# Cross-attention and feed-forward block: the attention loop taken in beats of two key blocks, with the subtraction of maxima and the sums of denominators on other engines

## The chip, the cores and the metric

The kernel runs on one NeuronCore of a Trainium2 chip. The metric is the device time of one execution in microseconds (us). In the profile the engines are PE (TensorE: matmuls; PEld is its loading of stationary operands), DVE (VectorE), ACT (ScalarE), POOL (GpSimd) and SP (SyncE). Each engine works through its own queue in program order. DMAs that add to what lies at their destination are issued from POOL's queue here.

## The reference, cut to what matters

All tensors are float32 with one batch. `x` is 2048 x 256, the context 1601 x 256 with a mask over its rows, and there are 4 heads of 64.

```python
latents = _layernorm(x)
xn, ln = layernorm(ctx, ln_x_g, ln_x_b), layernorm(latents, ln_l_g, ln_l_b)
q  = ln @ W_q
kv = concatenate([xn @ W_kv, ln @ W_kv], axis=1)      # 1601 + 2048 keys
qn, kn = rmsnorm(q, q_gamma) * 64 ** -0.5, rmsnorm(k, k_gamma)
sim  = where(full_mask, qn @ kn.T, -finfo.max)        # per head; latents are never masked
attn = softmax(sim)
x = x + (attn @ v) @ W_out + b_out
y = _layernorm(x)                                     # no gains
h = bit_linear(y, w1)                                 # rows to int8 steps, weights to -1, 0, 1
h = silu(depthwise_conv1d(h, conv_w, conv_b))         # 3 taps along the sequence
x = x + bit_linear(h, w2)
```

## The kernel before

A prologue (lines 207 to 409) normalizes context and latents, makes keys `kT` (two heads on the two halves of the partitions), values `v_sb` and queries `qT`, and looks ahead at the scores of the first unit. The middle is the attention loop. The end is the feed-forward part in slots (lines 794 to 963).

**Units and blocks.** A unit is 512 queries (of 2048, index `g`) and a pair of heads (`pr`): 8 units, numbered 0 to 7 here. Keys come in 29 blocks of 128: 13 of context (0 to 12, the last one padded) and 16 of latents (13 to 28). A tile of one unit and one block is 128 keys x 2 heads x 512 queries, [128 x 1024] float32.

**Softmax.** It needs each query's maximum before any exponential. So while unit u runs, `look_ahead` makes the scores of unit u+1 (`sa`, in PSUM) and DVE reduces each tile to maxima over 32 keys at a time (`mxs`). Context blocks are kept: ACT copies them to SBUF with the mask added (`sg`, in a ring of 14). Latent blocks are dropped and made again in unit u+1. At a unit's end `column_maxima`, `transpose_maxima`, `row_maxima` and `spread_shift` join the maxima (`m`, `tpm`, `nm`) and split their negatives in two bfloat16 parts (`hi`, `val`, `rows`). A matmul of `rows` with ones then spreads them over all key partitions (`sh`), and ACT copies that to SBUF (`nb`).

In unit u+1 a kept block gets its shift by `subtract` (`sg + nb`, on DVE). A latent block gets it on PE: `again` puts the bfloat16 matmul of `rows` into PSUM and adds the scores to it (`st`). `exponential` (ACT) makes `pt` in SBUF, in a pool of 5, two steps ahead. `attend` multiplies with the values into `ot`, one PSUM bank that all blocks of a unit add to. Every score matmul uses one half of the array's rows for each head, every product with values one half of its columns; the profile writes these as 64*128 and 128*64.

**PSUM.** Score tiles (`sa`, `st`, `sh`) share three buffers of two banks (`big`). One bank is for `ot`, one (`bank`) for everything small.

**Denominators.** Sums of `pt` over blocks are kept in two tiles. POOL adds context blocks and the last two blocks to `acc`; DMAs issued on POOL's queue add the other latent blocks to `acd` (in the last unit, DVE). `finish_unit` copies `ot` out (ACT) and puts small pieces on a plan by step: `join` the sums (POOL), eight matmuls to columns (`dn`), inverses (DVE), eight diagonal matrices (`dg`, ACT), eight matmuls that spread them again (`rd`), and the division (DVE).

**Order.** All four engines are held in program order (`InOrder`, lines 157 to 170). The loop runs over 8 x 29 steps of one block each. `order` takes a latent block in even steps and a context block in odd ones, then the last three latent blocks. `early` says which block of the next unit is looked ahead to in which step. After a query group's second unit, `finish_block` plans for each of its four blocks of 128 rows: bias (POOL), projection (`po`, PE), residual and statistics (DVE, `mv`), inverse deviation (two steps on POOL), normalization, quantization (DVE), transposes (`tpq`, PE) and a copy to `xq_all` (ACT). These pieces fall into units 2, 4, 6 and, for the last group, into the feed-forward slots. In the last unit `weight_tasks` load and quantize the feed-forward weights.

Of the kernel before, what the change touches and what calls it, by code (L numbers as in the profile page):

```python
# [17 lines left out]
P = 128  # L18
# [8 lines left out]
def kernel(  # L27
# [386 lines left out]
    def at(k, *calls):  # L414

        plan.setdefault(k, []).extend(calls)
# [30 lines left out]
    with att:  # L447
# [13 lines left out]
        def transpose_maxima(m4):  # L461
            tp = bank("tpm", [P, P])
            tensor.transpose(tp, m4.rearrange("p a b -> p (a b)"), ident)
            return tp

        def row_maxima(tp):
# [6 lines left out]
            vector.tensor_copy(hi, nm)  # L473
# [24 lines left out]
        def subtract(u, j):  # L498

            vector.tensor_tensor(staged[u, j], staged[u, j], shifts[u][1], ALU.add)  # L500
# [13 lines left out]
        def attend(u, j, pt, ot, sums, i):  # L514


            g, pr = units[u]
            acc, acd = sums
            if j < NCB or i >= NKB - 2:
                if j == 0:  # L520
                    gpsimd.tensor_copy(acc, pt)
                else:
                    gpsimd.tensor_tensor(acc, acc, pt, ALU.add)
            elif u == len(units) - 1:
                if i == 0:
                    vector.tensor_copy(acd, pt)
                else:
                    vector.tensor_tensor(acd, acd, pt, ALU.add)
            elif i == 0:
                gpsimd.dma_start(acd, pt)  # L530
            else:
                gpsimd.dma_start(acd, pt, accum_op=ALU.add)
            for hh in range(2):
# [3 lines left out]
                    start=(i == 0), stop=(i == NKB - 1),  # L537
                )

        def finish_unit(k, ot, sums, dst):  # L540

            scalar.copy(dst, ot)
# [6 lines left out]
            def denominators():  # L549

                box["dn"] = bank("dn", [P, NSUB, 2])
                for sub in range(NSUB):
                    for hh in range(2):
                        tensor.matmul(
                            box["dn"][:, sub, hh : hh + 1], acc[:, hh, ts(sub, P)], ones[:, 0:1],
                            start=True, stop=True,
                        )

            def inverses():
                box["r"] = sm.tile([P, NSUB, 2], F32, tag="r", name="r", bufs=2)  # L560
                vector.reciprocal(box["r"], box["dn"])

            def diagonals():
                box["dg"] = ptp.tile([P, NSUB, 2, P], F32, tag="pt", name="dg")
                for sub in range(NSUB):
                    for hh in range(2):
                        scalar.activation(
                            box["dg"][:, sub, hh, :], ident, AF.Copy,
                            scale=box["r"][:, sub, hh : hh + 1],
                        )  # L570

            def spread_inverses():
                box["rd"] = bank("rd", [P, NSUB, P])
                for sub in range(NSUB):
                    for hh in range(2):
                        tensor.matmul(
                            box["rd"][halves(hh), sub, :], ones[:, :DH], box["dg"][:, sub, hh, :],
                            start=True, stop=True,
                        )

            def divide():
                vector.tensor_tensor(
                    dst, dst, box["rd"].rearrange("p s q -> p (s q)"), ALU.mult
                )

            for n, call in (
                (1, join), (3, denominators), (4, inverses), (5, diagonals), (6, spread_inverses),
# [149 lines left out]
        for k in range(AHEAD + 1):  # L737
            if kept(k):
                subtract(*steps[k])
# [257 lines left out]
```

## Time and profile before

| what | value |
|---|---|
| median of 3 runs | 1016.02 us (1014.09 to 1018.25) |
| the profiled execution: its own time, its span | 1019.8 us, 1018.0 us |
| mean granted PE clock | 0.899 |
| busy PE, DVE, ACT, POOL | 859.8, 819.0, 523.0, 537.6 us |
| DMA queue of POOL (software_dynamic) | 51.39 MB, 25.8% of 16 engines' span |

A group's line has the engine, the operation, what it writes and reads with shapes, the count, busy time and mean, and the idle time just before with what ended it. Nearly all lines of the attention loop and the end carry L165, the helper that holds the order, so groups are told apart by their tiles. In a timeline the first two columns are start and length in us; a matmul's length includes its way through the array, so the time that one takes from the next is the difference of their starts. One float32 matmul shows as two records: `x4` is one tile for both heads.

### The profile page before, as it was taken

What the parts mean: (1) busy time and instruction counts of PE and PEld (TensorE: products, weight loads), DVE (VectorE), ACT (ScalarE), POOL (GpSimd) and SP (SyncE); (2) the same over time, 40 slices, a digit from 0 to 9 for tenths busy, and PEclk for the clock granted to TensorE, in tenths of its full rate; (3) what the DMA queues carried; (4) which work ended last, traced back from release to release, by engine and by line L of the source; (5) the groups of instructions that cost most, each with busy time, mean ns of one, the idle gap of its engine ahead of it and who ended that gap; (6) DMA issues with size and microseconds to landing.
All of it is one profiled execution on the core that took longest, in us unless ns stands there. A gap on an engine that the chain in (4) does not pass through costs nothing.

```text
span 1018.0 us, 10253 instructions
## 1 busy us (share of the span) xinstructions
PE 859.8 (84%) x3672; PEld 323.7 (32%) x3672; DVE 819.0 (80%) x946; ACT 523.0 (51%) x706; POOL 537.6 (53%) x415
## 2 busy tenths in 40 slices
PE   4788978998998999899899999989998877555543
PEld 3334532222322333232233323223332323333321
DVE  4566447996898689779868998977898995799996
ACT  2456444554654644455454566556554435755560
POOL 2432343556555556646655675646566546545431
PEclk9999998999999999899989999999998897556565
DMA  5010002453444344245534335544344000000000
GB/s 133 21 33 10 1 0 58 87 104 80 86 91 97 83 83 82 62 84 99 109 75 79 75 83 104 96 92 98 69 84 102 22 0 21 1 11 11 21 10 32
DMA packets 29775, 63.28 MB, mean 62 GB/s; under 512 B 7259, under 2 KB 16668, under 8 KB 29724
## 3 DMA queue, kind: packets, MB, share of 16 engines
q0 software_dynamic: 14112, 51.39, 25.8%
q1 hardware_dynamic: 12030, 10.44, 3.3%
q10 hardware_dynamic: 3582, 0.79, 0.4%
q8 instruction: 29, 0.48, 0.2%
q14 instruction: 22, 0.18, 0.1%
HBM read 9.13 MB, written 2.10 MB: 11 GB/s over the span
## 4 chain that ended last, share of the span: by engine, by line
PE 53%; DVE 36%; ACT 5%; issue 2%; POOL 2%; DMA 2%; ACTq 0%; POOLq 0%; DVEq 0%
PE sa L165 15%; PE ot L165 15%; PE st L165 10%; DVE mxs L165 6%; DVE sg L165 5%; PE kv L353 5%; DVE t L165 4%; DVE m L165 3%; PE sa L179 3%; DVE acd L165 2%; DVE y L165 2%; DVE h L165 2%; DVE hi L165 1%; DVE rows L165 1%; DVE hq L165 1%
## 5 line engine op out<-in xcount | busy, mean ns | idle before, releaser
L165 POOL TENSOR_TENSOR acc<-acc,pt 128x1024 f32<-128x1024 f32 x112 | 283.2, 2529 | 36.0 <-ACT pt L165 35.5
L165 PE MATMUL ot<-pt,v_sb 128*64 128x512 f32 x928 | 254.2, 633 | 2.0 <-ACT pt L165 1.9
L165 DVE TENSOR_TENSOR sg<-sg,nb 128x1024 f32<-128x1024 f32 x104 | 218.2, 2104 | 14.1 <-ACT nb L165 14.1
L165 PE MATMUL sa<-q_un,kT 64*128 64x512 f32 x812 | 223.9, 640 | 3.0 <-DVE mxs L165 3.0
L165 POOL DMA_DIRECT2D acd<-pt x98 | 84.0, 857 | 214.6 <-ACT pt L165 156.9
L165 ACT ACTIVATE sg<-sa,maskc 128x1024 f32<-128x1024 f32 x91 | 101.2, 1112 | 177.1 <-PE sa L165 176.9
L165 ACT ACTIVATE pt<-st 128x1024 f32<-128x1024 f32 x128 | 130.9, 1023 | 77.4 <-PE st L165 77.3
L165 DVE TRANSPOSE_TENSOR_REDUCE mxs<-sa 128x32 f32<-128x1024 f32 x112 | 137.2, 1231 | 34.4 <-PE sa L165 33.6
L165 DVE TRANSPOSE_TENSOR_REDUCE mxs<-sg 128x32 f32<-128x1024 f32 x91 | 112.7, 1238 | 40.8 <-ACT sg L165 40.8
L165 PE MATMUL st<-q_un,kT 64*128 64x512 f32 x512 | 141.8, 633 | 0.0
L165 ACT ACTIVATE pt<-sg 128x1024 f32<-128x1024 f32 x104 | 109.3, 1051 | 41.9 <-DVE sg L165 41.9
L165 PEld LDWEIGHTS sa<-q_un,kT 64*128 64x128 f32 x812 | 64.0, 186 | 138.7 <-issue 88.3
L165 PEld LDWEIGHTS ot<-pt,v_sb 128*64 128x64 f32 x928 | 48.8, 139 | 183.8 <-issue 174.1
L165 POOL TENSOR_TENSOR side<-side,t 128x512 f32<-128x512 f32 x32 | 40.6, 1270 | 48.8 <-DVE t L165 47.8
L165 PEld LDWEIGHTS st<-q_un,kT 64*128 64x128 f32 x512 | 53.4, 202 | 34.9 <-issue 31.1
L165 ACT ACTIVATE t<-h,cb_sb,cw_sb 128x256 f32<-128x256 f32 x64 | 37.9, 591 | 38.6 <-DVE h L165 38.6
L353 PE MATMUL kv<-wkv_sb,feat 128*128 128x512 f32 (+1 forms) x116 | 55.5, 620 | 0.0
L165 PE MATMUL st<-rows,ones 64*128 64x512 bf16 x256 | 52.4, 403 | 1.5 <-DVE mxs L165 1.5
L329 DVE TENSOR_TENSOR nn<-raw,ss 128x512 f32<-128x512 f32 (+1 forms) x23 | 15.7, 681 | 47.0 <-POOL ss L101 47.0
L165 PE MATMUL py<-w2T,hq 128*128 128x256 bf16 x128 | 30.2, 417 | 26.4 <-DVE hq L165 26.4
L101 POOL TENSOR_TENSOR ss<-ss,neg_half 128x8 f32<-128x8 f32 (+1 forms) x23 | 37.7, 1638 | 1.9
L97 POOL TENSOR_SCALAR ss<-ss 128x8 f32<-128x8 f32 (+1 forms) x23 | 5.8, 253 | 60.2 <-DVE ss L320 60.1
(130 smaller groups left out, 1001.1 us busy)
## 6 DMA issues: line engine op xcount, KB each, us to landing
acd<-pt POOLq DMA_DIRECT2D x98, 512.0 KB, 4.5
tok<-in_x_dram SPq DMA_DIRECT2D x4, 512.0 KB, 3.5
q_un<-in_x_dram SPq DMA_DIRECT2D x4, 512.0 KB, 3.6
w_sb<-in_L_ffn_w_dram SPq DMA_DIRECT2D x4, 512.0 KB, 3.2
out_dram<-res SPq DMA_DIRECT2D x16, 128.0 KB, 1.8
tok<-in_ctx_dram SPq DMA_DIRECT2D x3, 512.0 KB, 4.1
wkv_sb<-in_L_xattn_W_kv_dram ACTq DMA_DIRECT2D x1, 512.0 KB, 9.0
wo_sb<-in_L_xattn_W_out_dram SPq DMA_DIRECT2D x1, 256.0 KB, 8.8
```

The costliest lines, as they stand in the source:

```text
L97: gpsimd.tensor_scalar(x, x, floor, None, op)
L101: gpsimd.tensor_tensor(x, x, e, ALU.pow)
L165: return tc.keep_in_program_order(getattr(self.engine, name)(*args, **kwargs))
L179: tensor.matmul(st[:, hh, :], kT[halves(hh), pr, ts(j, P)], qT[g][halves(hh), pr, :], start=start, stop=True,)
L329: nc.vector.tensor_tensor(nn[:rows, :nb, :].rearrange("p b (h d) -> p b h d", d=DH), raw[:rows, :nb, :].rearrange("p b (h d) -> p b h d", ...
L353: nc.tensor.matmul(kv[:rows, b, :], feat[:, c, c0 + b * rows : c0 + (b + 1) * rows], wkv_sb[:, c, :], start=(c == 0), stop=(c == ND - 1),)
```

## The change

- The loop goes in beats of up to two blocks, 14 to a unit: 13 of a latent and a context block, and one of the last three latent blocks (26, 27, 28). In a beat come all scores (looking ahead for the next unit, and `again` for the next beat), then the planned pieces, then the products with values of both blocks. Three blocks are looked ahead to in seven beats, two in four; beats 11 to 13 have none. The exponentials of a beat are made one beat before, that of its context block first.
- POOL does `subtract`, two beats ahead of the block's product, at the end of a beat's program.
- The sums go in two chains of DMAs, latent blocks into `acc` and context blocks into `acd`. DVE adds the context block in beats 1, 4, 7, 10 and, in the last unit, in all beats but the first. In the last beat POOL adds blocks 26 and 28, DVE block 27.
- `denominators` is two matmuls with 64 columns of ones and 512 moving columns each; `divide` inverts the result in PSUM (DVE) and multiplies. Diagonals and the second spreading go. `ot` is copied out by DVE.
- `hi` is made by ACT; `tpm` uses a `big` buffer; `row_maxima` is cut in two, the second part `place_maxima`.
- The planned pieces fall on beats instead of steps; `residual` and `spread` go to the front of their beat's pieces.

The diff, cut to its core:

```diff
@@ -411,9 +411,10 @@
     plan = {}
-    def at(k, *calls):
-        plan.setdefault(k, []).extend(calls)
+    def at(k, call, first=False):
+        calls = plan.setdefault(k, [])
+        calls.insert(0 if first else len(calls), call)
     def quant_scales(amax, n, vector=nc.vector):
@@ -459,7 +460,7 @@
             return m4
         def transpose_maxima(m4):
-            tp = bank("tpm", [P, P])
+            tp = big("tpm")[:, 0, :P]
             tensor.transpose(tp, m4.rearrange("p a b -> p (a b)"), ident)
             return tp
@@ -470,7 +471,10 @@
                 nm, tp.rearrange("p (a i) -> p i a", a=4), AX.X, ALU.max, negate=True
             )
             hi = sm.tile([P, 32], BF16, tag="hi", name="hi", bufs=2)
-            vector.tensor_copy(hi, nm)
+            scalar.copy(hi, nm)
+            return nm, hi
+        def place_maxima(nm, hi):
             val = sm.tile([P, 32], F32, tag="val", name="val", bufs=2)
             vector.scalar_tensor_tensor(val, hi, second, nm, ALU.mult, ALU.add)
@@ -497,7 +501,7 @@
         def subtract(u, j):
-            vector.tensor_tensor(staged[u, j], staged[u, j], shifts[u][1], ALU.add)
+            gpsimd.tensor_tensor(staged[u, j], staged[u, j], shifts[u][1], ALU.add)
         def again(u, j):
@@ -511,35 +515,36 @@
             scalar.activation(pt, staged.pop((u, j)), AF.Exp)
             return pt
-        def attend(u, j, pt, ot, sums, i):
+        def attend(u, j, pt, ot, first, last):
             g, pr = units[u]
-            acc, acd = sums
-            if j < NCB or i >= NKB - 2:
-                if j == 0:
-                    gpsimd.tensor_copy(acc, pt)
-                else:
-                    gpsimd.tensor_tensor(acc, acc, pt, ALU.add)
-            elif u == len(units) - 1:
-                if i == 0:
-                    vector.tensor_copy(acd, pt)
-                else:
-                    vector.tensor_tensor(acd, acd, pt, ALU.add)
-            elif i == 0:
-                gpsimd.dma_start(acd, pt)
-            else:
-                gpsimd.dma_start(acd, pt, accum_op=ALU.add)
             for hh in range(2):
                 h = 2 * pr + hh
                 tensor.matmul(
                     ot[halves(hh), :], v_sb[:, j, h * DH : (h + 1) * DH], pt[:, hh, :],
-                    start=(i == 0), stop=(i == NKB - 1),
-                )
+                    start=first, stop=last,
+                )
+        def by_vector(u, b, n):
+            if b == NB - 1:
+                return n == 1
+            return n == 1 and (b % 3 == 1 or (u == len(units) - 1 and b > 0))
+        def add_up(u, b, n, pt, sums):
+            acc = sums[n % 2]
+            if by_vector(u, b, n):
+                vector.tensor_tensor(acc, acc, pt, ALU.add)
+            elif b == NB - 1:
+                gpsimd.tensor_tensor(acc, acc, pt, ALU.add)
+            elif b == 0:
+                gpsimd.dma_start(acc, pt)
+            else:
+                gpsimd.dma_start(acc, pt, accum_op=ALU.add)
         def finish_unit(k, ot, sums, dst):
-            scalar.copy(dst, ot)
+            vector.tensor_copy(dst, ot)
             box = {}
             acc, acd = sums
@@ -548,45 +553,18 @@
             def denominators():
-                box["dn"] = bank("dn", [P, NSUB, 2])
...
-                        )
+                box["dn"] = bank("dn", [P, QW])
+                for hh in range(2):
+                    tensor.matmul(
+                        box["dn"][halves(hh), :], ones[:, :DH], acc[:, hh, :],
+                        start=True, stop=True,
+                    )
             def divide():
-                vector.tensor_tensor(
...
-            ):
+                vector.reciprocal(box["dn"], box["dn"])
+                vector.tensor_tensor(dst, dst, box["dn"], ALU.mult)
+            for n, call in ((0, join), (1, denominators), (2, divide)):
                 at(k + n, call)
@@ -639,10 +617,10 @@
                 gpsimd.tensor_tensor(x1[qb], x1[qb], bo_sb, ALU.add)
             for n, call in (
-                (-2, bias), (0, project_out), (1, residual), (2, inverse_deviation), (3, normalize),
-                (5, quantize), (6, transpose), (7, spread),
+                (-1, bias), (0, project_out), (1, residual), (1, inverse_deviation), (2, normalize),
+                (3, quantize), (3, transpose), (4, spread),
             ):
-                at(k + n, call)
+                at(k + n, call, call in (residual, spread))
@@ -711,81 +689,95 @@
             calls += [lambda c=c: transpose_w1(box1, c) for c in range(ND)]
             calls += [lambda c=c: transpose_w2(box2, c) for c in range(2)]
             for n, call in enumerate(calls):
-                at(k + n, call)
+                at(k + n // 2, call)
         assert NKB == 29 and NCB == 13
-        order = [NCB + i // 2 if i % 2 == 0 else i // 2 for i in range(2 * NCB)]
...
-        spread_shift(0, row_maxima(transpose_maxima(column_maxima(0))))
+        beats = [[NCB + i, i] for i in range(NCB)] + [list(range(2 * NCB, NKB))]
+        NB = len(beats)
+        AHEAD = NCB - 2
+        early = [[0, 1, 2]] + [[i + 2] for i in range(1, AHEAD)]
+        latents = iter(range(NCB, NKB))
+        for i in range(1, AHEAD):
+            early[i] += [next(latents) for _ in range(1 if i in (2, 5, 7, 10) else 2)]
+        assert next(latents, None) is None
         pts = {}
-        def kept(k):
...
-                pts[k] = exponential(*steps[k])
+        def unit_beat(k):
+            u, b = divmod(k, NB)
+            return (u, b, beats[b]) if u < len(units) else (u, b, [])
+        def subtract_all(k):
+            u, _, blocks = unit_beat(k)
+            for j in blocks:
+                if j < NCB:
+                    subtract(u, j)
+        spread_shift(0, place_maxima(*row_maxima(transpose_maxima(column_maxima(0)))))
+        subtract_all(0)
+        subtract_all(1)
+        for j in beats[0]:
+            if j >= NCB:
+                again(0, j)
+            pts[0, j] = exponential(0, j)
         oT = mx = ot = sums = None
-        for k, (u, j) in enumerate(steps):
-            i = k % NKB
+        for k in range(len(units) * NB):
+            u, b, blocks = unit_beat(k)
+            v, _, following = unit_beat(k + 1)
             g, pr = units[u]
             ahead = u + 1 < len(units)
-            if i == 0:
+            if b == 0:
                 if pr == 0:
                     oT = wk.tile([P, NPAIR, QW], F32, tag="oT", name="oT")
                 ot = ps_o.tile([P, QW], F32, tag="ot", name="ot")
                 sums = [acp.tile([P, 2, QW], F32, tag=t, name=t) for t in ("acc", "acd")]
                 if not ahead:
-                    weight_tasks(k + 8)
...
-            if ahead and i == DONE:
+                    weight_tasks(k + 4)
+            pieces = plan.pop(k, [])
+            for n, j in enumerate(blocks):
+                if not by_vector(u, b, n):
+                    add_up(u, b, n, pts[u, j], sums)
+            if ahead and b == AHEAD:
                 mx = column_maxima(u + 1)
-            attend(u, j, pts.pop(k), ot, sums, i)
-            if ahead:
-                if i == DONE:
-                    mx = transpose_maxima(mx)
-                if i == DONE + 1:
-                    spread_shift(u + 1, mx)
-            for call in plan.pop(k, []):
+            for j in following:
+                if j < NCB:
+                    pts[v, j] = exponential(v, j)
+            looks = [look_ahead(u + 1, j) for j in early[b]] if ahead and b < AHEAD else []
+            for n in range(max(1, len(looks))):
+                for part in looks[n : n + 1]:
+                    list(part)
+                if n == 0:
+                    for j in following:
+                        if j >= NCB:
+                            again(v, j)
+                            pts[v, j] = exponential(v, j)
+            if ahead and b == AHEAD + 1:
+                spread_shift(u + 1, mx)
+            for call in pieces:
                 call()
-            if i == NKB - 1:
+            for n, j in enumerate(blocks):
+                attend(u, j, pts[u, j], ot, (b, n) == (0, 0), (b, n) == (NB - 1, len(blocks) - 1))
+            for n, j in enumerate(blocks):
+                if by_vector(u, b, n):
+                    add_up(u, b, n, pts[u, j], sums)
+                del pts[u, j]
+            if ahead and b == AHEAD:
+                mx = place_maxima(*row_maxima(transpose_maxima(mx)))
+            subtract_all(k + 2)
+            if b == NB - 1:
                 finish_unit(k + 1, ot, sums, oT[:, pr, :])
                 if pr == NPAIR - 1:
                     nc.sync.dma_start(
                         q_un[g].rearrange("p (s d) -> p s d", d=D), x_t[:, ts(g, NSUB), :]
                     )
                     for sub in range(NSUB):
-                        finish_block(k + 9 - (not ahead) + 4 * sub, g * NSUB + sub, oT, sub)
+                        finish_block(k + 5 + 2 * sub, g * NSUB + sub, oT, sub)
@@ -957,7 +949,7 @@
     unit_rows(0)
     unit_rows(1)
     for s in range(last + NP + 4):
-        for call in plan.pop(len(steps) + s, []):
+        for call in plan.pop(len(units) * NB + s, []):
             call()
         slot(s)
     assert not plan
```

## The prediction

> **What bounds the kernel now.** I read the page first (the chain that ended last, the costly groups), then the table by stage, then PE's, DVE's and POOL's timelines inside single units.
>
> From the page, the chain by engine and two groups (columns: count, busy us, mean ns, idle before):
>
> ```profile
> PE 53%; DVE 36%; ACT 5%; issue 2%; POOL 2%; DMA 2%; ACTq 0%; POOLq 0%; DVEq 0%
> L165 POOL TENSOR_TENSOR acc<-acc,pt 128x1024 f32<-128x1024 f32 x112 | 283.2, 2529 | 36.0 <-ACT pt L165 35.5
> L165 DVE TENSOR_TENSOR sg<-sg,nb 128x1024 f32<-128x1024 f32 x104 | 218.2, 2104 | 14.1 <-ACT nb L165 14.1
> ```
>
> The table by stage, cut where a unit's `nb` is copied (stretch; length; busy PE, PEld, DVE, ACT, POOL; granted clock; DMA share; GB/s):
>
> ```profile
> 243.30:327.60 84.30, 81.09 (x366) 25.81 (x366) 69.52 (x50) 46.58 (x53) 48.43 (x30) 0.99 0.47 94
> 327.60:422.60 95.00, 88.68 (x387) 29.19 (x383) 80.66 (x90) 48.08 (x56) 57.76 (x42) 0.95 0.40 78
> 776.30:858.80 82.50, 68.01 (x305) 24.03 (x305) 68.28 (x52) 38.05 (x47) 46.99 (x23) 0.83 0.08 26
> ```
>
> The cuts are at 162.4, 243.3, 327.6, 422.6, 510.0, 602.0, 683.0, 776.3 and 858.8 us. Units 0 to 6 are full of PE; units 2, 4, 6 (95, 92, 93 us) also carry the four row blocks finished for the query group before. Unit 7 has no scores to look ahead to and is bound by DVE and POOL.
>
> PE's timeline in unit 1, one pair of blocks, then two products in a row in unit 7:
>
> ```profile
> 272.72 0.38 PE L165 MATMUL st<-rows,ones 64*128 64x512 bf16 x2
> 272.94 1.02 PE L165 MATMUL st<-q_un,kT 64*128 64x512 f32 x4
> 273.89 1.08 PE L165 MATMUL ot<-pt,v_sb 128*64 128x512 f32 x4
> 274.90 1.13 PE L165 MATMUL sa<-q_un,kT 64*128 64x512 f32 x4
> 275.96 1.08 PE L165 MATMUL ot<-pt,v_sb 128*64 128x512 f32 x4
> 276.97 1.13 PE L165 MATMUL sa<-q_un,kT 64*128 64x512 f32 x4
> 277.93 0.38 PE L165 MATMUL st<-rows,ones 64*128 64x512 bf16 x2
> ...
> 783.17 1.94 PE L165 MATMUL ot<-pt,v_sb 128*64 128x512 f32 x8
> 785.04 0.39 PE L165 MATMUL st<-rows,ones 64*128 64x512 bf16 x2
> ```
>
> From start to start: shift 0.22, st to ot 0.95, ot to a score 1.01, sa to ot 1.06, sa to shift 0.96; a pair is 5.21. Two ot in a row take 1.87, so the first takes 0.86: changing between scores (64*128) and products (128*64) costs 0.1 to 0.2.
>
> The end of unit 2 on DVE and PE, and on POOL three of the DMA sums in unit 3 and one block's finish in unit 2:
>
> ```profile
> 416.01 2.69 DVE L165 CAST hi<-nm 128x32 bf16<-128x32 f32 x1
> 418.74 2.38 DVE L165 SCALAR_TENSOR_TENSOR val<-hi,second,nm 128x32 f32<-128x32 bf16 x1
> 421.90 0.61 PE L165 MATMUL sh<-rows,ones 64*128 64x512 bf16 x2 [4.14 <-DVE rows L165]
> ...
> 475.25 0.87 POOL L165 DMA_DIRECT2D acd<-pt  x1 [3.34 <-DMA acd<-pt]
> 480.32 0.87 POOL L165 DMA_DIRECT2D acd<-pt  x1 [1.82 <-DMA acd<-pt]
> ...
> 379.84 0.18 DVE L165 BATCH_NORM_AGGREGATE mv<-st 128x2 f32<-128x6 f32 x1
> 380.12 1.10 POOL L165 TENSOR_SCALAR mv<-mv 128x1 f32<-128x1 f32 x1 [3.49 <-DVE mv L165]
> ```
>
> Small DVE steps take over 2 us beside POOL's adds and PE waits 4.1; one chain of DMA sums can issue only every 5.07 us; POOL waits in order for a block's variance. Now POOL can afford that: nobody on the path needs its adds soon.
>
> **What PE gains.** Before, a unit is 12 pairs of 5.21, four extra sa of 0.86, one sa, st, ot of 3.1, three st, ot of 2.18 and a last ot of 1.0: 76.6, with tpm and sh 77.1. After, a beat is sa 0.96, shift 0.22, st 0.90 (in its mode, between 0.86 and 0.95), sa 1.06, ot 0.86, ot 1.01 = 5.01, and 5.87 with a third sa. Of beats 0 to 10 seven have three sa and four have two: 61.1. Beats 11 to 13 (no looking ahead) are 3.3, 5.5 and 3.9 with tpm and sh. Sum 73.8: 3.3 less in each of units 0 to 6. Denominators: dn took 1.88 (257.73 to 259.61) and rd 0.97; the two wide matmuls are one ot's work, 0.95: 1.9 less in units 1 to 6. The eight diagonals (2.4 of ACT) go; the wide reciprocal on DVE is 0.5 to 0.9 by the 128x1 and 128x8 ones (164 and 169 to 173 ns), and DVE, which loses thirteen subtracts of 2.1 a unit, hides it: nothing. The rows of shifts: PE waited 22.9 in all for them, in six of seven units, and ran at half clock for some 2 more each time (st 1.91 for 1.02 after them): 35. After, three st (3.4) lie between tpm and sh, and hi goes to ACT; nm 0.3, hi 0.3, val 0.9, rows 0.7 to 1.9 fit under that: the wait goes.
>
> **What POOL then holds up.** A subtract on POOL is taken at 2.4 (its adds of the same size: 2.33 least, 2.45 median); 2.3 and 2.6 are the bounds. In a plain beat POOL issues one or two DMAs (0.87 each) and subtracts: 4.2 of 5.0 to 5.9, and runs about a beat ahead. The engines of DMA: 25.8% of 1018 us over 98 sums is 2.7 us each; two in a beat are 5.4. Beats 1 to 10 hold 16 sums, 43 us of 56, and a chain at 5.07 per sum needs 51: covered, narrowly. If that cover goes, see the rivals. Two places are not covered.
>
> (1) The start of a unit. nb is ready when ACT has done the exponentials of blocks 26 to 28 and the copy: 8.9 us after beat 11 began on PE (beat 11 3.3, three st 3.4, then exponential 28 and copy 1.0 each). POOL then does, in its order: subtract of block 0, the adds of blocks 26 and 28, subtract of block 1: 4 x 2.45 = 9.8, so 18.7. ACT's exponential of block 1 (1.05) stands in front of the copies of beat 0's scores, so sa 0 leaves PSUM at 20.9 (1.11). PE finished beat 13 at 12.7 and used its three buffers for sa, st, sa by 15.7; the third sa waits for the first one's buffer: 5.2 lost. Join (2.35), two DMA issues and the subtract of block 2 follow, 0.7 more in beat 1. After such an idle the clock drops as above: 2. Together 7.9, in units 1 to 6: 47.
>
> (2) The row blocks, units 2, 4, 6. In beats 5, 7, 9 POOL's queue holds, ahead of the subtract for two beats on, the inverse deviation, which waits for DVE, and DVE does the residual only after that beat's maxima. From beat 5's start: sa's second done 3.0, maxima (1.23 each) 4.65, residual and statistics (0.42, 0.43, 0.18) 5.7; POOL's two steps (1.1, 0.57) 7.4, the next block's bias (0.72) 8.1, subtract 10.5. Beat 6 began at 5.0; ACT's exponential there ends at 6.6 of it, the copy at 7.7, and the third sa, due at 3.0, waits 4.8. The same in beat 8 (4.7); beat 10 has two sa and loses 2.1. With two drops of the clock: 15.6 a unit, 47 in all. Before, this wait of POOL's (34.4 in all) held up only its own adds.
>
> [...] The trace has the same add at 2.33 on POOL and at 1.17 on DVE at its least, though DVE's mean is 2.10, as it waits for POOL. [...]
>
> **Unit 7.** No looking ahead, the second chain is DVE's. POOL: 9.8 to the second subtract, DMA issues and join to 16.3, then sums 1 to 12 every 5.07: the twelfth issues at 72 and lands at 76.7 (4.5), two adds to 81.5, the cm of the feed-forward part (2.4), tpu and copy: 86 against 82.5. So 3 later. The feed-forward stage keeps its DVE work (140 of 159): 0, within 3 either way; its blocks come earlier in its slots.
>
> **The sum.** Units: 74; three of 73.8 + 0.95 + 7.9 = 82.6; three with 5.1 of projections and transposes and 15.6 more = 103.3; 86. That is 718 for the stretch that took 696.4: 21 longer. The profiled execution took 1019.8 (span 1018.0), 3.8 above the median of 1016.0; 1016 + 21 is about 1036.
>
> **Rivals.** A: the unit start stalls, the row blocks do not (DVE's residual falls between maxima, or the beats after have slack): 47 less, 989. For it: POOL ran ahead before; against: the residual is queued behind the maxima in program order. B: POOL keeps ahead at both places, and PE's 5.01 and 5.87 decide: 942. That needs the subtract of block 1 within 4 us of nb, where its queue holds 9.8; it decides if the adds of 26 and 28 do not stand in front. C: the DMA chains decide. If each sum of a chain waits for one of the other (2.7 behind 5.07 = 7.8), each two-sum beat (eight a unit) is 2 or more over PE's; over seven units some 110, half of it in stalls already counted: 1090. It decides once a beat's two landings take longer than the beat before; 0.47 of DMA share with one chain speaks for, the 16 of 5.4 above against. D: the stalls come but the clock holds: twelve drops of 2 less, 1012.
>
> **How the numbers follow.** Forecast 0.50 (own range 1014 to 1062, from subtracts of 2.3 to 2.6, clock drops of 1 to 3, and 3 either way in the last stage), A 0.20, B 0.12, C 0.10, D 0.08. Half a per cent, 5 us, is about what a measurement here can tell. Faster: A, B, a little of D and of the forecast's lower end, 0.36; within: 0.10; slower 0.54. Leaving out B and most of C gives 972 to 1066.
>
> **What would show it.** Right: ot in runs of two with 0.86 between; no wait of sh for rows; on PE an idle of about 5 before the third sa of beat 0; POOL in the order subtract, add, add, subtract after each nb, and ACT waiting for POOL's sg by 60 us or more in all; in units 2, 4, 6 POOL's mv steps ahead of a late subtract, and units of about 103 beside 83. Wrong: even units no longer than 90 (A), PE over 95% busy with no such waits (B), or POOL's sums waiting mostly for DMA (C).

## The result, and the profile after

| | before | after |
|---|---|---|
| median | 1016.43 us (1014.09 to 1018.25, 4 runs) | 1059.93 us (1055.84 to 1061.92, 4 runs) |
| the profiled execution: its own time, its span | 1019.8, 1018.0 us | 1055.84, 1054.1 us |
| mean granted PE clock | 0.899 | 0.874 |

The changed kernel is slower: ratio 1.0424, interval 1.0386 to 1.0462, or 43.5 us. The two profiled executions lie only 36.0 apart: the one of before is 3.4 above its median, the one of after 4.1 below. What follows explains the 36; the other 7.5 is how the two profiled executions fell.

From the page of after, the busy times, the chain by engine and the costliest group of PE:

```profile
PE 827.6 (79%) x3448; PEld 320.8 (30%) x3448; DVE 648.0 (61%) x876; ACT 501.9 (48%) x642; POOL 592.8 (56%) x485
DVE 12%; DMA 4%; PE 3%; POOL 2%; issue 1%; ACT 1%; POOLq 0%; DVEq 0%; ACTq 0%
L165 PE MATMUL sa<-q_un,kT 64*128 64x512 f32 x812 | 221.7, 639 | 51.4 <-ACT sg L165 44.9
```

PE has 32 us less to do than before and DVE 171 less, and yet the span is 36 longer: PE's idle time rose from 158 to 227 us. The chain's shares add up to 23% only, so this chain was not followed past the last quarter of the span. It says nothing of the loop, and the reading has to go by waits and by stages. The last line already says where PE waits: 44.9 us of its idle time come before scores, for ACT to empty a buffer (`sg`).

Two more of the waits of after (engine and tile that waited, and for what; total us, times, longest):

```profile
ACT pt L165 <- POOL sg L165: 191.9, 73, 7.6
PE tpq L165 <- DVE yq L165: 44.1, 13, 7.3
```

ACT waits 192 us for POOL's subtracts (60 or more had been named as the sign), and PE waits as long at the transposes `tpq` as for scores (27.8 of the 44.1 in units 2, 4 and 6, the rest at the row blocks of the last query group). POOL waits 65.3 for `mv` and 103.2 for its DMA sums (71.6 for those into `acc`, 31.6 for those into `acd`).

The stages of after, cut where a unit's `nb` is copied, for units 1, 2 and 7 (columns as before: length; busy PE, PEld, DVE, ACT, POOL; granted clock; DMA share; GB/s):

```profile
236.90:319.70 82.80, 76.13 (x337) 25.64 (x337) 47.80 (x42) 44.07 (x46) 57.12 (x39) 0.94 0.71 140
319.70:428.10 108.40, 88.50 (x353) 30.18 (x351) 59.08 (x83) 44.60 (x48) 63.77 (x51) 0.87 0.60 119
803.70:893.00 89.30, 63.42 (x283) 20.80 (x280) 57.03 (x40) 35.70 (x39) 59.49 (x39) 0.86 0.49 107
```

All units, in us:

| unit | 0 | 1 | 2 | 3 | 4 | 5 | 6 | 7 | the rest |
|---|---|---|---|---|---|---|---|---|---|
| before | 80.9 | 84.3 | 95.0 | 87.5 | 89.8 | 83.6 | 92.9 | 82.5 | 321.6 |
| predicted | 74 | 82.6 | 103.3 | 82.6 | 103.3 | 82.6 | 103.3 | 86 | 321.6 |
| after | 75.3 | 82.8 | 108.4 | 81.0 | 105.9 | 81.2 | 107.5 | 89.3 | 322.7 |

The row of before is cut where `nb` is copied. The prediction's cut at 602.0 lies 2.2 us behind that copy, which starts at 599.84, so its 92.0 and 81.0 for units 4 and 5 are 89.8 and 83.6; its sum uses only the whole stretch.

Units 0, 1, 3 and 5 came within 1.6 us of the forecast, and gain 16 on before. The loss lies in units 2, 4 and 6, the ones with row blocks: 44 us longer than before, where 32 were forecast.

Two plain beats of unit 0 on PE, and `sh` at that unit's end:

```profile
196.05 1.13 PE L165 MATMUL sa<-q_un,kT 64*128 64x512 f32 x4
...
199.04 1.94 PE L165 MATMUL ot<-pt,v_sb 128*64 128x512 f32 x8
200.91 1.13 PE L165 MATMUL sa<-q_un,kT 64*128 64x512 f32 x4
...
206.63 1.13 PE L165 MATMUL sa<-q_un,kT 64*128 64x512 f32 x4
...
234.32 0.38 PE L165 MATMUL sh<-rows,ones 64*128 64x512 bf16 x2
```

From start to start, a beat with two `sa` takes 4.86 us (5.01 forecast) and one with three 5.72 (5.87); the products come in runs of two, and `sh` has no wait for `rows`, where PE had waited 4.1 before.

The start of unit 1, across engines:

```profile
238.02 2.35 POOL L165 TENSOR_TENSOR sg<-sg,nb 128x1024 f32<-128x1024 f32 x1 [0.96 <-ACT nb L165]
240.34 5.63 POOL L165 TENSOR_TENSOR acc<-acc,pt 128x1024 f32<-128x1024 f32 x2
245.94 2.33 POOL L165 TENSOR_TENSOR sg<-sg,nb 128x1024 f32<-128x1024 f32 x1
248.30 1.06 ACT L165 ACTIVATE pt<-sg 128x1024 f32<-128x1024 f32 x1 [5.65 <-POOL sg L165]
...
250.41 2.08 PE L165 MATMUL sa<-q_un,kT 64*128 64x512 f32 x4 [6.58 <-ACT sg L165]
```

This is the order forecast: subtract, add, add, subtract, then ACT's exponential, then (left out here, 249.26) the copy that empties PE's buffer, then PE. PE's wait is 6.58, and the eight records of products behind it take 3.68 for the usual 1.94: the granted clock is 0.50 from 252.4 to 256.1, and 1.00 in the 3.9 us after.

POOL at one row block of unit 2, then PE at the row blocks of that unit:

```profile
368.29 0.24 POOL L165 TENSOR_SCALAR mv<-mv 128x1 f32<-128x1 f32 x1 [4.46 <-DVE mv L165]
...
374.47 1.13 PE L165 MATMUL sa<-q_un,kT 64*128 64x512 f32 x4 [4.11 <-ACT sg L165]
...
386.47 0.39 PE L165 MATMUL tpq<-ident,yq 128*128 128x128 bf16 x2 [3.31 <-DVE yq L165]
...
405.78 0.28 PE L165 MATMUL tpq<-ident,yq 128*128 128x128 bf16 x2 [3.58 <-DVE yq L165]
...
419.65 0.28 PE L165 MATMUL tpq<-ident,yq 128*128 128x128 bf16 x2 [2.37 <-DVE yq L165]
```

The wait for scores that was forecast for beat 6 is there (4.11 for 4.8): POOL stands 4.46 for `mv`, subtracts late, and ACT has waited 6.50 for that subtract. Those of beats 8 and 10 are not (in unit 4 there is one of 1.11 in beat 8). In their place PE itself stands at the transposes: 9.26 for `yq` and 0.54 for the projection behind one of them. The transposes share one PSUM bank and stand in PE's queue ahead of the products with values, so the wait stops everything on PE. This is the wait that the prediction had not seen.

### The profile page after: what moved, and what is told of

Same layout as the page of the kernel before. It is cut to its first block, busy times and chain, and to the rows that moved or that the text cites. A ratio compares the mean times of both kernels' runs of the same rounds, so it can differ in the third digit from the quotient of the medians.

```text
span 1054.1 us, 9664 instructions
## 1 busy us (share of the span) xinstructions
PE 827.6 (79%) x3448; PEld 320.8 (30%) x3448; DVE 648.0 (61%) x876; ACT 501.9 (48%) x642; POOL 592.8 (56%) x485
## 5 line engine op out<-in xcount | busy, mean ns | idle before, releaser
L165 POOL TENSOR_TENSOR sg<-sg,nb 128x1024 f32<-128x1024 f32 x104 | 274.7, 2642 | 33.2 <-ACT nb L165 33.1
L165 PE MATMUL sa<-q_un,kT 64*128 64x512 f32 x812 | 221.7, 639 | 51.4 <-ACT sg L165 44.9
L165 PE MATMUL ot<-pt,v_sb 128*64 128x512 f32 x928 | 248.8, 663 | 6.4 <-ACT pt L165 6.3
L165 POOL DMA_DIRECT2D acc<-pt x104 | 94.4, 908 | 109.0 <-DMA acc<-pt 71.6
L165 PE MATMUL st<-q_un,kT 64*128 64x512 f32 x512 | 132.3, 594 | 0.0
L165 DVE TRANSPOSE_TENSOR_REDUCE mxs<-sa 128x32 f32<-128x1024 f32 x112 | 132.1, 1209 | 0.0
L165 PEld LDWEIGHTS sa<-q_un,kT 64*128 64x128 f32 x812 | 72.9, 192 | 186.1 <-issue 95.0
L165 DVE TENSOR_TENSOR acd<-acd,pt 128x1024 f32<-128x1024 f32 x48 | 73.4, 1528 | 66.1 <-DMA acd<-pt 56.7
L165 PEld LDWEIGHTS ot<-pt,v_sb 128*64 128x64 f32 x928 | 61.9, 147 | 159.0 <-issue 137.5
L165 POOL DMA_DIRECT2D acd<-pt x64 | 56.2, 878 | 69.2 <-DVE acd L165 37.5
L329 DVE TENSOR_TENSOR nn<-raw,ss 128x512 f32<-128x512 f32 (+1 forms) x23 | 15.6, 680 | 46.8 <-POOL ss L101 46.8
L165 POOL TENSOR_TENSOR acc<-acc,pt 128x1024 f32<-128x1024 f32 x16 | 39.5, 2468 | 4.4 <-ACT pt L165 3.8
```

Source lines behind the costliest of these rows:

```text
L165: return tc.keep_in_program_order(getattr(self.engine, name)(*args, **kwargs))
L329: nc.vector.tensor_tensor(nn[:rows, :nb, :].rearrange("p b (h d) -> p b h d", d=DH), raw[:rows, :nb, :].rearrange("p b (h d) -> p b h d", ...
```

## Experiments

Each edit is against the changed kernel unless said otherwise. Ratios are against the kernel before, run on the same chip beside it (medians 1015.85 to 1016.92). The changed kernel was not run again beside them: its 1059.93 stands beside a median of 1016.43. Four questions were asked: what holds the row blocks, what holds the start of a unit, whether the subtract on POOL is the fault, and what the wide denominators are worth alone.

### The row blocks: later inverse, earlier quantization, both

The first kernel moves the inverse deviation one beat later, the second the quantization one beat earlier, the third does both.

```diff
-                (-1, bias), (0, project_out), (1, residual), (1, inverse_deviation), (2, normalize),
-                (3, quantize), (3, transpose), (4, spread),
+                (-1, bias), (0, project_out), (1, residual), (2, inverse_deviation), (2, normalize),
+                (2, quantize), (3, transpose), (4, spread),
```

Later inverse alone:

> The changed kernel with the inverse deviation planned one beat later, so that POOL no longer waits in its queue for DVE's statistics; the quantization and its transposes stay in one beat. Order theory (POOL's and PE's in-order waits are the price): in units 2, 4, 6 the wait of about 4.1 us for a buffer in beat 6 goes with the slow clock after it, while PE's waits for yq (9.3 us a unit) stay: those units fall from 107 to about 101, the total by some 18 to about 1042. DMA theory (two chains on the same DMA engines make the sums late and with them everything on POOL): nothing changes, 1060.

Measured 1047.88 us (2 runs), ratio 1.0309 (1.0227 to 1.0390). Units 2, 4, 6 are 103.2, 104.2, 102.1. In unit 2 the wait for scores in the row blocks is gone, and the waits at the transposes grew from 3.31, 3.58, 2.37 to 4.59, 4.00, 2.44. The three units are 12.3 shorter together. That is three times the wait of 4.11, but since the waits at the transposes grew meanwhile, it is what the edit gained and not the whole price of POOL's wait for `mv`.

Earlier quantization alone:

> The changed kernel with the quantization planned one beat earlier (beside the normalization), so that the transposes find it done; POOL's wait for the statistics stays. Order theory: PE's waits for yq (9.3 us a unit in units 2, 4, 6) go, but POOL's late subtracts then show in beats 6, 8 and 10 as the prediction had them (4.8, 4.7, 2.1): even units about 103, total about 1046. DMA theory: 1060.

Measured 1048.05 us (2 runs), ratio 1.0310 (1.0234 to 1.0386). The waits at unit 2's transposes fell to 2.06, 2.33 and 0.20, but they now name DVE's `q_un`, the residual, and no longer `yq`. The wait of beat 6 stayed at 4.11, and the last block's projection, which waits for ACT to copy the transposes out of the bank (`xq_all`), stood 2.94 for 0.54.

Both:

> Both pieces moved. Order theory: units 2, 4, 6 keep only their projections and transposes over an odd unit's 82, so about 88 instead of 107; three times 19 less, about 1003. DMA theory: the even units are long because POOL's sums land late; they stay above 100 and the total above 1045.

Measured 1045.39 us, ratio 1.0283 (1.0225 to 1.0342); units 2, 4, 6 are 100.9, 99.9, 102.9. Some 40 us too slow for the expectation. PE's first two waits at the transposes of unit 2 in this kernel, and before them DVE:

```profile
377.50 0.30 DVE L165 TENSOR_SCALAR yq<-y 128x256 bf16<-128x256 f32 x1
...
378.88 1.21 DVE L165 TRANSPOSE_TENSOR_REDUCE mxs<-sa 128x32 f32<-128x1024 f32 x1
380.01 0.39 DVE L165 TENSOR_TENSOR q_un<-po,q_un 128x256 f32<-128x256 f32 x1
...
380.45 0.27 PE L165 MATMUL tpq<-ident,yq 128*128 128x128 bf16 x2 [4.03 <-DVE q_un L165]
...
398.33 0.37 PE L165 MATMUL tpq<-ident,yq 128*128 128x128 bf16 x2 [3.47 <-DVE q_un L165]
```

`yq` is ready in time, and PE waits as long. What it waits for is the bank: the next block's projection `po` has been in it since the beat before, and it comes free when DVE reads it in `residual`, which DVE does only after the beat's maxima (380.01, when `yq` has been ready since 377.80). `yq` and the bank are late for the same reason, so mending either alone uncovers the other. That suggests one step: the residual ahead of the maxima.

### The residual at the front of DVE's beat

`residual` (DVE) and `spread` (ACT) are issued at the very start of their beat, before any score's maxima, and the quantization goes one beat earlier. The inverse deviation stays where the change put it.

```diff
-    plan = {}
+    plan, plan_first = {}, {}
...
-        calls = plan.setdefault(k, [])
-        calls.insert(0 if first else len(calls), call)
+        (plan_first if first else plan).setdefault(k, []).append(call)
...
-                (3, quantize), (3, transpose), (4, spread),
+                (2, quantize), (3, transpose), (4, spread),
...
+            for call in plan_first.pop(k, []):
+                call()
...
```

> The changed kernel with the residual and the copy to xq_all issued at the start of their beat, before its scores' maxima, and the quantization one beat earlier. With both pieces moved only (1045), PE's transposes still waited 4 us: their one PSUM bank is held by the next block's projection until DVE, after the beat's maxima, has added it. Theory: PE's wait in its own queue for that bank and for yq is the term the prediction lacked; with it and POOL's wait gone, units 2, 4, 6 fall from 107 to about 88 and the total by 45 to 57, to 1003 to 1015. If the even units are long for another reason (POOL's sums, the wide inverse of 3.3 us on DVE), they stay above 97 and the total above 1030.

Measured 1005.73 us (1004.67 to 1006.64), ratio 0.9899 (0.9845 to 0.9953): 54 us less than the changed kernel, and less than before. The earlier quantization alone had given 12 of that; `residual` and `spread` were not moved one without the other. The only wait that is left at unit 2's transposes on PE:

```profile
402.52 0.27 PE L165 MATMUL tpq<-ident,yq 128*128 128x128 bf16 x2 [2.60 <-DVE q_un L165]
```

Units 2, 4 and 6 are 91.4, 88.5 and 88.7 for 108.4, 105.9 and 107.5: 53 us, all that the median lost. PE's waits behind the start of these units fell from 42.8 to 8.0 in all, and its busy time from 259.4 to 241.7, as the granted clock rose with them (in unit 2 from 0.87 to 0.93): some two thirds of the gain are waits, one third is the clock. The wait for scores at the row blocks is down to 0.70. POOL's wait for `mv`, which the prediction blamed, needed no step of its own: with the residual early, the variance is early.

### The start of a unit: order or amount

First the order. In the last beat POOL subtracts for two beats on before it adds.

```diff
+            if b == NB - 1:
+                subtract_all(k + 2)
...
-            subtract_all(k + 2)
+            if b < NB - 1:
+                subtract_all(k + 2)
```

> The changed kernel, but in a unit's last beat POOL does the subtract of the next unit's block 1 before its adds of blocks 26 and 28. Nothing is added or removed. Order theory: the subtract comes 4.7 us earlier, the wait of the third score matmul at a unit's start falls from 6.6 to about 2 and the clock stays up: some 6 less in each of units 1 to 6, about 1024. Speed theory (POOL is simply slower at subtracting, 2.6 for 2.1, and short of time in every beat): the work is the same, so the adds only delay the next subtracts instead; 1055 or more. DMA theory: 1060.

Measured 1053.38 us, ratio 1.0360 (1.0308 to 1.0412); 1024 had been expected. In unit 1 the wait of 6.58 became 0.70 and 4.27; in unit 2 there are 2.90, 0.82 and 1.40. The wait moved by a beat and shrank little: the adds stand ahead of the next subtract in any order.

Then the amount. DVE takes the two adds of the last beat and the join.

```diff
             if b == NB - 1:
-                return n == 1
+                return True
...
-                gpsimd.tensor_tensor(acc, acc, acd, ALU.add)
+                vector.tensor_tensor(acc, acc, acd, ALU.add)
```

> The changed kernel with the adds of blocks 26 and 28 and the join of the two sums on DVE instead of POOL (7.2 us of POOL's work at each unit's start go; nothing else moves). Putting the subtract ahead of the adds only moved the wait from beat 0 to beats 1 and 2, so the theory is now: POOL's whole work between nb and the subtract of block 2, 16 us, is the price, not its order. Then the subtracts of blocks 1 and 2 come 4.9 and 7.2 earlier, PE's wait of 6.6 falls to about 2 and no other takes its place: some 6 in each of units 1 to 6, about 1022. If it is DMA landings that hold POOL, 1050 or more.

Measured 1027.81 us (1026.15 to 1031.03), ratio 1.0111 (1.0045 to 1.0178): 32 less than the changed kernel. Units 1, 3 and 5 are 79.5, 76.0 and 75.4, for 82.8, 81.0 and 81.2; units 2, 4 and 6 gave 7 more. In unit 1 what is left of PE's wait is 0.32, 1.98, and 1.00 for DVE's copy of `oT`. So it was mostly three [128 x 1024] instructions on POOL, and less where they stood, that the start of a unit paid for.

### The subtract back on DVE

```diff
-            gpsimd.tensor_tensor(staged[u, j], staged[u, j], shifts[u][1], ALU.add)
+            vector.tensor_tensor(staged[u, j], staged[u, j], shifts[u][1], ALU.add)
```

> The changed kernel with the subtracts back on DVE, all else as changed. Theory (POOL's queue holds up the subtracts): the wait at a unit's start goes but for 1 or 2, as does that of beat 6, while PE's waits for yq and the bank stay (9 a unit in units 2, 4, 6): some 6 less in six units and 6 in three, about 1005. DMA theory: 1050 or more. If DVE is then late with its maxima (13 more steps of 1.2 to 3.4 a unit), the units go to 85 and the total to about 1030.

Measured 1131.47 us (2 runs), ratio 1.1137 (1.1043 to 1.1231), where a gain had been expected: 72 slower than the changed kernel, although the subtract itself is cheaper, 1.2 us for 2.64. By its waits, ACT stands 344.3 us for DVE's subtracts, and PE 83.2 for ACT's copies. One beat of it, on DVE and PE:

```profile
282.68 1.22 DVE L165 TENSOR_TENSOR sg<-sg,nb 128x1024 f32<-128x1024 f32 x1
...
286.19 2.08 PE L165 MATMUL sa<-q_un,kT 64*128 64x512 f32 x4 [6.07 <-ACT sg L165]
...
287.33 2.34 DVE L165 TRANSPOSE_TENSOR_REDUCE mxs<-sa 128x32 f32<-128x1024 f32 x2
289.60 1.18 DVE L165 TENSOR_TENSOR sg<-sg,nb 128x1024 f32<-128x1024 f32 x1
```

DVE's subtract stands behind the maxima of its beat, these behind ACT's copy of the beat's scores, the copy behind ACT's exponential, and that behind the subtract. The engines form a ring and go round it once a beat: 6.9 us from one subtract to the next, where PE needs 4.9 to 5.7. POOL takes twice as long for the subtract but has no maxima in its queue, so it breaks the ring. That the subtract is on POOL is not the fault of the change; with this order of work it is what holds the beats together. A subtract on DVE ahead of the beat's maxima was not tried.

### The wide denominators alone, in the kernel before

The old kernel, with the two wide matmuls and the inversion in PSUM in place of columns, diagonals and spreading; the pieces fall on steps 1, 3 and 4.

```diff
-                box["dn"] = bank("dn", [P, NSUB, 2])
...
+                box["dn"] = bank("dn", [P, QW])
+                for hh in range(2):
+                    tensor.matmul(
+                        box["dn"][halves(hh), :], ones[:, :DH], acc[:, hh, :],
+                        start=True, stop=True,
+                    )
...
+                vector.reciprocal(box["dn"], box["dn"])
+                vector.tensor_tensor(dst, dst, box["dn"], ALU.mult)
```

> The kernel before with the wide denominators alone (two matmuls of 512 columns, an inverse of 128x512 on DVE in PSUM, no diagonals, no second spreading; the pieces at steps 1, 3 and 4). Theory of the prediction: PE does 1.9 less in each of units 1 to 6, 11 in all, and the inverse is hidden: about 1005. Rival: in the kernel before DVE has 70 to 81 of 81 to 95 us busy, and the inverse (3.35 in the changed kernel's trace, where 0.5 to 0.9 was estimated) holds the maxima behind it, so PE waits for score buffers: 2 to 3 back a unit, 1014 to 1018.

Measured 1015.69 us (1013.46 to 1020.59, 10 runs), ratio 1.0006 (0.9975 to 1.0038): nothing. The inversion on DVE and the next shift on PE, in its unit 1:

```profile
263.40 3.33 DVE L165 RECIPROCAL dn<-dn 128x512 f32<-128x512 f32 x1
...
268.67 0.39 PE L165 MATMUL st<-rows,ones 64*128 64x512 bf16 x2 [1.63 <-DVE mxs L165]
```

The wide matmuls cost PE the 0.95 forecast (from 258.89 to the next start at 259.84). The reciprocal takes 3.33, not 0.5 to 0.9, and holds back the maxima, and PE waits 1.63 for them: nearly all of the 1.9 is handed back. Over the whole kernel PE's waits of `st` for maxima are 11.3 us, where they were 1.5 before. In the changed kernel the same reciprocal takes 3.33 too (3.37 in the last unit), but PE has no wait for maxima there in the loop, where DVE no longer has the subtracts.

### The two remedies together, and the last unit

The residual first together with the adds and the join on DVE. This was run after the kernel "All on DVE" below, of which its expectation speaks:

> The pieces' order and the adds and join on DVE together, with unit 7 as in the changed kernel. In the run of all three, units 0 to 6 took 564 us and unit 7 grew from 89 to 99 because one add on DVE waited 26.5 us while POOL did 11 subtracts without a pause. Theory: with DMA issues between the subtracts again, unit 7 is back at 85 to 89 (its chain of sums at 5.07 a beat) and the total falls from 991 to about 980. If unit 7 was long for another reason (DVE's weight pieces), it stays near 99.

Measured 973.7 us (972.09 to 977.03, 6 runs), ratio 0.9593 (0.9559 to 0.9627): the fastest version. Against the changed kernel it is 86.2 less, the sum of the two remedies alone (54.2 and 32.1). POOL still waits 101.4 for its DMA sums, for 103.2 in the changed kernel. Units 0 to 7 are 74.3, 79.7, 84.0, 79.0, 82.3, 78.7, 85.2 and 85.5.

Two kernels went after the last unit on top of that. In one DVE adds both blocks of every beat there but the first, in the other by turns with the DMAs, the latent block in odd beats:

```diff
-            return n == 1 and (b % 3 == 1 or (u == len(units) - 1 and b > 0))
+            if u == len(units) - 1:
+                return b > 0
+            return n == 1 and b % 3 == 1
```

```diff
-            return n == 1 and (b % 3 == 1 or (u == len(units) - 1 and b > 0))
+            if u == len(units) - 1:
+                return b > 0 and (n == 1 or b % 2 == 1)
+            return n == 1 and b % 3 == 1
```

All on DVE:

> The two before together, and in unit 7 DVE adds both blocks of every beat but the first. Theory: units 1, 3, 5 about 76, units 2, 4, 6 about 82, unit 7 about 72 (no chain of sums at 5.07 a beat): 74 + 228 + 246 + 72 = 620 where the changed kernel took 731, so about 950. If the two chains of DMAs decide as soon as the waits are gone, a unit cannot fall under about 82: 1000 or more.

Measured 990.86 us (988.63 to 992.68, 4 runs), ratio 0.9752 (0.9696 to 0.9808), with unit 7 at 98.8. What happened to one add of DVE's there, beside POOL:

```profile
733.92 26.48 DVE L165 TENSOR_TENSOR acc<-acc,pt 128x1024 f32<-128x1024 f32 x1
...
734.01 25.30 POOL L165 TENSOR_TENSOR sg<-sg,nb 128x1024 f32<-128x1024 f32 x11
...
761.14 3.57 PE L165 MATMUL ot<-pt,v_sb 128*64 128x512 f32 x8 [28.55 <-DVE oT L165]
```

With its DMAs gone, POOL does the remaining eleven subtracts without a break, and DVE's add, 1.2 us by itself, lasts until the last of them is through. PE waits 28.55 for the copy behind it.

By turns:

> As the kernel before in this list, but in unit 7 the latent blocks are added by DMA in even beats and by DVE in odd ones, so that POOL's subtracts are parted by DMA waits in every second beat and the chain of sums no longer needs 5.07 a beat. Theory: unit 7 falls to 70 to 78, the total to about 965. If POOL's back-to-back subtracts starve DVE here too, an add of DVE lasts over 7 us and unit 7 stays at 85 or more.

Measured 979.55 us (978.02 to 983.15, 6 runs), ratio 0.9650 (0.9616 to 0.9684), with unit 7 at 91.2 for 85.5. DVE's adds in unit 7 are again held beside POOL's subtracts, now in pairs: three in a row, from 726.16 on, took 3.32, 3.37 and 5.83 (3.33, 3.38 and 3.54 without this edit), and PE waits 7.89 for the copy behind them, for 5.62. Two more took 7.29 together; behind them stands `part`, a sum over the weights, for which PE waits 5.1 here and not at all without the edit. No single add lasts over 5.97, where one over 7 had been named as the sign.

In the last unit POOL's waits for its DMAs are what keeps it from crowding DVE out; both attempts took some of them away and lost. For the first the add of 26.48 shows it; for the second it is read from these two waits, and no run separates it.

## Why the prediction was right or wrong

The prediction had the direction, both places where POOL is not covered, and a range that holds the time, by 2 us at its upper end. The size was short: 1036 for 1059.93, so 20 us longer was forecast and 43.5 measured.

**What held.** PE's gain: the beats are 0.15 shorter than worked out, and unit 0 is 75.3 for 74, with a wait of 2.86 for scores at its start that was not forecast. The wait for `rows` is gone. The start of a unit, step (1): 6.58 measured in unit 1 and 6.00 in two pieces in unit 2, for 5.2 and 0.7, through the queue order forecast, and 35.0 over units 1 to 6 for 35.4. That its price is mostly the amount of POOL's work was shown by moving it; rival B's condition, that the adds do not stand in front of the subtract, was not enough. Odd units came out at 81.0 to 82.8 for 82.6. The chains of DMA sums, rival C, are not what decides, although the sign named for C came: POOL waits 103.2 for them, more than for all else that its sums wait for. With both remedies it waits 101.4 for the same chains, in a kernel 86 us faster.

**The step that failed is (2), the row blocks**: 15.6 a unit. Measured in unit 2, the waits of PE after the unit's start are 4.11 + 3.31 + 3.58 + 0.54 + 2.37 = 13.9, for 11.6 forecast; in units 4 and 6 they are 15.0 and 13.9. The sum is not far off, but the mechanism is right for beat 6 only. The step followed POOL's queue and left out PE's: the change puts quantization and transposition in the same beat, and lets the next block's `po` take the one bank a beat before the transposes need it, so that PE itself, in order, waits for DVE. That POOL gets back ahead while PE is stopped there, so that the two later stalls that were forecast do not come, is only argued; it fits that with earlier quantization, where PE stands less, a wait for scores of 0.93 to 1.00 stands in beat 8 of all three units, where the changed kernel has one in unit 4 alone.

The second part of this term, the clock, was somewhat short: PE is busy 88.5 in unit 2 and 76.1 in unit 1, 12.4 more, of which 5.1 is the added work; 7.3 is the slower clock (0.87 for 0.94), where 4 was allowed. Waits and clock make 21.2 for 15.6, and the unit is 5.1 longer than forecast. Units 4 and 6, each against the unit before it, give 2.1 and 5.2 for the clock by the same working. Over the three units the waits are 8.0 longer than forecast and the clock takes 2.6 more, of the 11.9 by which these units exceed the forecast. That both kinds of wait come from the residual behind the maxima was shown by the kernel that moves it, with `spread` and the quantization: 53 of the 54 us that it gained lie in these three units, and the earlier quantization alone gained 12.

**Unit 7** is 89.3 for 86. The interval of POOL's sums was right (5.02 to 5.11, but two gaps of 6.08 and 6.57), and the second subtract ended 10.5 after `nb` was there, for 9.8; the twelfth sum was issued 75.4 after the unit began, for 72, and the last two adds took 5.84 for 4.8.

**The feed-forward part** cost 1.9, inside the 3 allowed. **The reciprocal** was mis-sized by a factor of four to seven: small ones were scaled, and those do not show what the wide one takes. From 0.164 us for one element a partition to a median of 0.169 for eight, an element adds under 1 ns; from 0.164 to 3.33 for 512 it is some 6.2 ns (both estimates, from these times). Its step, "hidden, nothing", held all the same in the changed kernel, where DVE is busy 61% of the span, and failed where the edit stood alone.

**The sum.** The terms of the forecast add to 717.7, which is 21.3 longer and makes 1037, not 1036; the 8.9 of step (1) adds to 8.7. The stretch from unit 0 to 7 took 731.4, and 696.4 before; of the 13.7 missing, 11.9 is step (2), 3.3 unit 7, 1.3 unit 0, and the odd units gave 2.8 back. To the 35.0 that the stretch lost, 1.1 outside it brings the 36 between the profiled executions. The forecast added its difference to the median of before, and the executions of after lie higher than its profiled one: 7.5 more.

**The slower engine.** The least times of the same add on POOL and on DVE, as the prediction has them, gave the right sign for one instruction: 2.64 us for a subtract on POOL in the mean (2.33 at least) and 1.2 on DVE. The prediction had taken 2.4, and its upper bound of 2.6 lies under the mean. For the kernel the sign was the other one, since the same subtract moved to DVE made it 72 us slower. What the instruction cost here was what stood before and behind it in the queue.

**The expectations that missed.** Both shifts of pieces together (1045 for 1003) missed the bank; the subtract first (1053 for 1024) took an amount for an order; the subtract on DVE (1131 for a gain) missed the ring; the adds of the last unit on DVE (991 for 950, and 980 for 965) missed that POOL, once it no longer waits, crowds DVE out.

## What to carry to other kernels

When a loop is recast in coarser steps, write down for each piece of work that is moved both what its engine waits for and which shared buffer it needs at that step, and do it for every in-order queue, not only the one that received new work: here the engine on the path stopped at a small transpose that shared a bank. Small work on which a slower chain hangs (a residual, a variance) goes ahead of a beat's bulk work, not behind it: here that was worth 54 us, with the quantization a beat earlier. An engine that takes twice as long for an instruction can still be the better place for it, if it breaks a ring of waits (here 2.64 us on POOL for 1.2 on DVE, in a kernel 72 us faster); and taking a wait away from an engine is worth checking for whom it now crowds out (here one add of 26.48 us for 1.2).

## What the runs showed of the hardware

- One DVE add of two SBUF operands beside eleven back-to-back two-input instructions on POOL took 26.48 us in place of 1.2 ("All on DVE"): it ended 1.1 us after the last of them. Beside pairs of subtracts three such adds took 3.32, 3.37 and 5.83 ("By turns").
- A DVE reciprocal of [128 x 512] float32 in PSUM took 3.33 to 3.37 us, some 6.2 ns an element by the estimate above, where the two-input multiply of the same size behind it took 0.69.
- After PE had waited, products took nearly twice as long: the eight records of two `ot` 3.68 us after the wait of 6.58, for 1.94, at a granted clock of 0.50 for 1.00 in the 3.9 us after them.
